# A two-stream scan kernel: the upper channels of the reverse stream convolved by taps on VectorE, b*s moved to GpSimd, one add of u, a new bank plan

## The chip, the cores and the metric

The kernel runs on one NeuronCore of one Trainium2 chip. The metric is the device time of one execution in microseconds (us), the median of several runs. The engines are called TensorE (PE in the profile, PEld its weight loads), VectorE (DVE), ScalarE (ACT) and GpSimd (POOL).

## The reference, cut to what matters

```python
# x: (4, 128, 96, 96) fp32; four sequences per image (rows and columns, each forwards and backwards)
t = grouped1x1(groupnorm(seq), in_proj)           # 4 groups, 128 -> 512 channels
u, gate = t[:, :256], t[:, 256:]
u = depthwise_conv(silu(u), dw_w)                 # 5 taps along the sequence, 256 channels
s = ssm_in @ u                                    # 32 channels
a = clip(DMIN + (DMAX - DMIN) * sigmoid(delta @ u), 1e-4, 0.9999)    # DMIN 0.999, DMAX 0.9999
b, c = tanh(B @ u), tanh(C @ u)
h = scan(h * a + b * s)                           # along the sequence
u = u + ssm_out @ (c * h + d * s)
y = out_proj @ grouped1x1(u * sigmoid(gate), mix) # then summed over the four sequences by fuse
```

Everything is fp32.

## The kernel before

The forward and the reverse stream run side by side. A *step* is 16 rows of both streams, cut by position modulo 4; a *pair* is one of the four positions p of a step in both streams, 384 columns each. There are 192 pairs. Each engine has its fixed order of instructions in a pair; the back part (gate, output, sum) lags six pairs behind the front. The depthwise convolution is done in two ways: on TensorE with banded 128x32 weights, or *by taps*: one ScalarE and four VectorE operations on the shifted silu. Only one of the four half-streams (forward, channels 128 to 255) went by taps.

```python
def by_taps(s, j):                # s: stream, j: half of the 256 channels
    return s == 0 and j == 1

GATE, FRONT, CONV_R, Y_F, SMALL = (0, 1), (2, 3), (0, 1), 2, 3      # PSUM banks
SSM, PROJ, Y_R, CONV_F = (4, 6), (5, 4), 6, 7

def conv(un, j):                  # by band: 8 matmuls and a copy
    ...
    for k in range(2):
        for g in range(4):
            mm(pc, g, band[:, j, un["p"], k, g, :], sil[:, j, g, k : k + N], k == 0, k == 1)
    nc.scalar.copy(un["u"][:, j, :], pc[:, :N])

def taps(un, ks):                 # by taps
    ...
        if k == 0:
            nc.scalar.activation(part, src, AF.Copy, scale=w_tap[:, 0:1])
        else:
            nc.vector.scalar_tensor_tensor(
                part, src, w_tap[:, k : k + 1], part, ALU.mult, ALU.add)

def ssm_out(bi):                  # after the matmuls, for each stream:
    ...
        nc.vector.tensor_add(pz, pz, bu["u"])
        nc.vector.scalar_tensor_tensor(gv, gv, 1.0, pz, ALU.add, ALU.mult)

def inputs(i):                    # for the pair before
    nc.scalar.activation(ta[:, p, :], bank(PROJ[0])[:, :N], AF.Tanh, bias=b_proj[:, 0:1])
    nc.gpsimd.tensor_scalar(a, a, half, DMIN + half, ALU.mult, ALU.add)
    nc.gpsimd.tensor_scalar(a, a, 0.9999, 0.0001, ALU.min, ALU.max)
    nc.vector.tensor_mul(ta[0:64, p, :], bank(PROJ[1])[64:P, :N], ta[0:64, p, :])   # b*s

def outputs(step, p):             # c*h + d*s, and a copy to the other partitions
    nc.gpsimd.tensor_mul(ta[64:P, p, :], tb[0:64, p, :], ta[0:64, p, :])
    nc.gpsimd.tensor_add(tb[64:P, p, :], ta[64:P, p, :], tb[64:P, p, :])
    nc.gpsimd.tensor_copy(tb[0:64, p, :], tb[64:P, p, :])
```

Of the kernel before, what the change touches and what calls it, by code (L numbers as in the profile page):

```python
# [35 lines left out]
P = 128  # L36
# [7 lines left out]
R = 4  # L44
# [9 lines left out]
def conv_preact_kernel(  # L54
# [58 lines left out]


    psum = ps.tile([P, 8, 512], F32, name="psum")
    GATE, FRONT, CONV_R, Y_F, SMALL = (0, 1), (2, 3), (0, 1), 2, 3
    SSM, PROJ, Y_R, CONV_F = (4, 6), (5, 4), 6, 7

# [41 lines left out]
    def stats_finish(b):  # L160
# [27 lines left out]
        nc.vector.tensor_scalar_mul(bn[:, 2:4], bn[:, 2:4], 0.5)  # L188
        bs = sp.tile([P, 2, 4], F32, tag="bsilu", name=f"bsilu_{b}")
        for q in range(R):  # L190
            for g in range(4):
                nc.gpsimd.tensor_copy(
                    bs[32 * q : 32 * q + 32, :, g], bn[32 * g : 32 * g + 32, 0:2]
                )
# [51 lines left out]

    band = wp.tile([P, 2, R, 2, 4, 32], F32, name="band")
    w_fin = wp.tile([P, 4, 2, P], F32, name="w_fin")
    b_fin = wp.tile([P, 1], F32, name="b_fin")
    with tc.tile_pool(name="prep", bufs=1) as pp:  # L250
        w_dw = load(dw_v, [P, 2, 4, 8], "w_dw", pp)
        id32 = pp.tile([P, 32], F32, name="id32")
        ident = pp.tile([P, P], F32, name="ident")
        make_identity(nc, ident)
        for q in range(R):
            r = slice(32 * q, 32 * q + 32)
            nc.gpsimd.tensor_copy(id32[r, :], ident[r, r])
        for j in range(2):
            for p in range(R):
                for k in range(2):  # L260
                    for g in range(4):
                        m = R * k - p + R - 1
                        nc.gpsimd.tensor_scalar_mul(
                            band[:, j, p, k, g, :], id32, w_dw[:, j, g, m : m + 1]
                        )

# [50 lines left out]

    def by_taps(s, j):
        return s == 0 and j == 1

    sils = {}

    def rows(i, bi, front_banks=FRONT):

        if i is not None:
            step, k = divmod(i, UB)
            s, g = divmod(k, 4)
            un = units[step * UB + s]
            wn, bn, bsil = stats[un["b"]]
            if g == 0:  # L330
                sils[step, s] = wk.tile(
                    [P, 2, 4, N + 1], F32, tag=f"sil{s}", name=f"sil_{step}_{s}"
                )
            sil = sils[step, s]
        if bi is not None:
            bu = units[bi]
            gwn, gbn, _ = stats[bu["b"]]
            gq, off = gate_at(bu)
        for c in range(4):
            for j in range(2):  # L340
                if i is not None:
                    r = slice(32 * j, 32 * j + 32)
                    m, q = (c, g) if by_taps(s, j) else (g, c)
                    mm(bank(front_banks[j]), c, wn[r, 32 * m : 32 * m + 32], x_in[s][r, q, :],
                       True, True)
                if bi is not None:
                    r = slice(64 + 32 * j, 96 + 32 * j)
                    mm(bank(GATE[j]), c, gwn[r, 32 * c : 32 * c + 32],
                       x_in[bu["s"]][r, gq, off : off + N], True, True)
        if bi is not None:  # L350
            gv = wk.tile([P, 2, N], F32, tag="gv", name=f"gv_{bu['id']}")
            for j in range(2):
                nc.scalar.activation(  # L353
                    gv[:, j, :],
                    bank(GATE[j])[:, :N],
                    AF.Tanh,
                    bias=gbn[:, 2 + j : 3 + j],
                    scale=0.5,
                )
            load_gate(bi + UB)  # L360
            bu["v"] = gv
        if i is not None:
            for j in range(2):
                nc.scalar.activation(  # L364
                    sil[:, j, g, :],
                    bank(front_banks[j])[:, : N + 1],
                    AF.Silu,
                    bias=bn[:, j : j + 1] if by_taps(s, j) else bsil[:, j, g : g + 1],
                )
            if g == 3:  # L370
                for j in range(2):
                    tap = by_taps(s, j)
                    if un["st"] == 0:
                        r, q = (slice(0, P), slice(0, 2)) if tap else (slice(0, 64), slice(0, 4))
                        nc.gpsimd.memset(sil[r, j, q, 0:1], 0.0)
                    if un["st"] == NS - 1:
                        r, q = (slice(0, P), slice(2, 4)) if tap else (slice(64, P), slice(0, 4))
                        nc.gpsimd.memset(sil[r, j, q, N : N + 1], 0.0)
                load_front(step + 1, s)

    def ssm_out(bi):

        pair = units[bi], units[bi + 1]
        z, p = scans[pair[0]["step"]][1], pair[0]["p"]
        for c in range(4):
            for s in range(2):
                for j in range(2):
                    r = slice(64 * j + 32 * s, 64 * j + 32 * s + 32)
                    mm(bank(SSM[s] + j), c, w_so[r, 128 * j + 32 * c : 128 * j + 32 * c + 32],
                       z[r, p, :], True, True)  # L390
        for s, bu in enumerate(pair):
            pz, gv = psum[:, SSM[s] : SSM[s] + 2, :N], bu["v"]
            nc.vector.tensor_add(pz, pz, bu["u"])  # L393
            nc.vector.scalar_tensor_tensor(gv, gv, 1.0, pz, ALU.add, ALU.mult)  # L394

    def conv(un, j):
        sil = sils[un["step"], un["s"]]
        pc = bank(CONV_R[j] if un["s"] else CONV_F)
        for k in range(2):
            for g in range(4):  # L400
                mm(pc, g, band[:, j, un["p"], k, g, :], sil[:, j, g, k : k + N], k == 0, k == 1)
        nc.scalar.copy(un["u"][:, j, :], pc[:, :N])  # L402

    def new_u(un):
        un["u"] = wk.tile([P, 2, N], F32, tag="u", bufs=2 * LAG + 2, name=f"u_{un['id']}")

    def taps(un, ks):
        sil, j = sils[un["step"], un["s"]], 1
        for k in ks:
            off, q = divmod(un["p"] + k, R)  # L410
            src, part = sil[:, j, q, off : off + N], un["u"][:, j, :]
            if k == 0:
# [8 lines left out]

    def proj(i, which):

        un = units[i]
        step, p = un["step"], un["p"]
        if step not in scans:
# [4 lines left out]
        ta, tb = scans[step]  # L431
        pp = bank(PROJ[which])
        cols = (qb, qb, qa, qa) if which == 0 else (qc, qc, qs, qs)
        for j in range(2):
            for c in range(4):
                mm(pp, c, w_proj[:, j, cols[c]], units[i + c % 2]["u"][:, j, :], j == 0, j == 1)
        if which == 1:
            nc.scalar.activation(  # L438
                tb[0:64, p, :], pp[0:64, :N], AF.Tanh, bias=b_proj[0:64, 1:2]
            )  # L440
            nc.scalar.activation(tb[64:P, p, :], pp[64:P, :N], AF.Copy, scale=d_sb[64:P, :])

    def inputs(i):

        un = units[i]
        ta, p = scans[un["step"]][0], un["p"]
        nc.scalar.activation(ta[:, p, :], bank(PROJ[0])[:, :N], AF.Tanh, bias=b_proj[:, 0:1])  # L447
        a = ta[64:P, p, :]
        half = (DMAX - DMIN) / 2
        nc.gpsimd.tensor_scalar(a, a, half, DMIN + half, ALU.mult, ALU.add)  # L450
        nc.gpsimd.tensor_scalar(a, a, 0.9999, 0.0001, ALU.min, ALU.max)  # L451
        nc.vector.tensor_mul(ta[0:64, p, :], bank(PROJ[1])[64:P, :N], ta[0:64, p, :])  # L452

# [53 lines left out]
    def pair(t):  # L507
        i, k, bi = 2 * t, t % R, 2 * (t - LAG)
        conv_here = i < NU
        front = i + UB if i + UB < NU else None  # L510
        back = 0 <= bi < NU
        if 0 <= i - 2 < NU:
            inputs(i - 2)
        rows(front, bi if back else None)
        if 0 <= bi - 2 < NU:
            accumulate(units[bi - 1])
        if conv_here:
            conv(units[i], 0)
        if k < 2 and 0 <= t // R - 1 < NU // UB:
# [4 lines left out]
        if conv_here:  # L524
            un = units[i]
            if un["order"] == "V" and un["b"] + 1 < B:
                stats_chunk(un["b"] + 1, un["st"] * R + k)
                if un["st"] == NS - 1 and k == R - 1:
                    later[:] = [stats_finish(un["b"] + 1)]
        if front is not None or back:  # L530
            rows(None if front is None else front + 1, bi + 1 if back else None)
        if back:
            ssm_out(bi)
        if conv_here:
            new_u(units[i + 1])
            for j in range(2):
                conv(units[i + 1], j)
        if back:
            accumulate(units[bi])
        if later:  # L540
            next(later[0], None)
        if i + 2 < NU:
            new_u(units[i + 2])
            taps(units[i + 2], range(K))
        if conv_here:
            proj(i, 1)
            proj(i, 0)

    for _ in stats_finish(b0):
        pass  # L550
    for i in range(UB):
        rows(i, None, (2 * (i % 2), 2 * (i % 2) + 1))
    new_u(units[0])
    taps(units[0], range(K))
    with tc.manual_schedule(
# [73 lines left out]
```

## Time and profile before

| | before |
|---|---|
| median | 2466.55 us (3 runs, 2462.74 to 2468.8) |
| TensorE, VectorE, ScalarE, GpSimd busy | 97%, 76%, 64%, 43% |
| four pairs | 49.2 us (order V: the sequences along the columns), 47.8 us (order H: along the rows) |

The busy shares, the chain and the costliest groups are shown in the prediction. One more view: the waits of GpSimd and of VectorE in the kernel before (who waited for whom: us in total, times, longest).

```profile
POOL t L450 <- ACT t L447: 1190.2, 189, 15.0
DVE psum L393 <- PE psum L314: 247.5, 133, 3.6
DVE t L465 <- POOL t L451: 18.5, 48, 1.0
```

GpSimd stands idle for 1190 us until ScalarE's tanh comes, and VectorE waits for TensorE ahead of the add of u.

### The profile page before, as it was taken

Reading aid. Unit: us, or ns where it says so; the run is one execution under the profiler, and the core shown is the slowest. Engines: PE = TensorE matmul, PEld = TensorE weight load, DVE = VectorE, ACT = ScalarE, POOL = GpSimd, SP = SyncE. Lnnn points to the kernel's source line nnn. Section 1 sums busy time; section 2 is a strip of 40 time slices with the busy share of each in tenths; the row PEclk is TensorE's granted clock in tenths of the full one; section 3 lists DMA queues with packets and bytes.
Section 4 is the critical chain, followed back from the end, with each engine's and each line's share of the span. In section 5 each row is a group of like instructions: output and inputs, shape, how many; then the busy total and the mean of one; then the engine's idle time right before and its main releaser. Section 6 shows DMA issues by size and latency. Waiting matters only on the chain.

```text
span 2461.1 us, 89876 instructions
## 1 busy us (share of the span) xinstructions
PE 2389.1 (97%) x40016; PEld 913.3 (37%) x40016; DVE 1859.2 (76%) x2343; ACT 1572.8 (64%) x2912; POOL 1051.3 (43%) x1170
## 2 busy tenths in 40 slices
PE   6999999999999999999999999999999999999997
PEld 3333333333333333333333333333333333333331
DVE  3688777777887787777877788777777777777774
ACT  4666676666666666666665666666666666666641
POOL 4344444444444444444443444444443444444441
PEclk9999999999999999999999999999999999999997
DMA  5212111113332211111342211111232111111111
GB/s 140 56 47 54 47 41 32 38 31 89 98 100 52 54 44 34 35 38 31 93 139 55 54 46 41 31 38 31 52 120 89 31 38 33 38 31 38 25 45 56
DMA packets 79283, 134.21 MB, mean 55 GB/s; under 512 B 11440, under 2 KB 73392, under 8 KB 78896
## 3 DMA queue, kind: packets, MB, share of 16 engines
q1 hardware_dynamic: 76704, 127.64, 19.3%
q8 instruction: 314, 5.14, 0.9%
q10 hardware_dynamic: 2192, 0.83, 0.1%
q14 instruction: 73, 0.60, 0.1%
HBM read 109.55 MB, written 18.87 MB: 52 GB/s over the span
## 4 chain that ended last, share of the span: by engine, by line
PE 82%; DVE 9%; POOL 3%; ACT 3%; issue 1%; DMA 0%; DVEq 0%; SPq 0%
PE psum L314 82%; DVE t L465 4%; ACT t L447 2%; DVE gv L394 2%; DVE psum L393 2%; POOL t L450 1%; POOL t L451 1%; DVE u L415 0%; DMA out<-acc 0%; DVE bn L310 0%; DMA acc<-in_xr 0%; ACT gv L353 0%; ACT L364 0%; ACT L438 0%; ACT sil L364 0%
## 5 line engine op out<-in xcount | busy, mean ns | idle before, releaser
L314 PE MATMUL psum<-sil,band 128*32 128x384 f32 x9216 | 821.6, 488 | 0.0
L450 POOL TENSOR_SCALAR t<-t 64x384 f32<-64x384 f32 x192 | 186.3, 970 | 1190.4 <-ACT t L447 1190.2
L314 PE MATMUL psum<-gv,w_fin 128*32 128x384 f32 x6144 | 582.9, 497 | 31.0 <-DVE gv L394 29.0
L393 DVE TENSOR_TENSOR psum<-psum,u 128x768 f32<-128x768 f32 x384 | 369.3, 962 | 248.3 <-PE psum L314 247.5
L314 PE MATMUL psum<-u,w_proj 128*32 128x384 f32 x6144 | 533.0, 486 | 0.0
L415 DVE SCALAR_TENSOR_TENSOR u<-sil,w_tap,u 128x384 f32<-128x384 f32 x768 | 478.9, 624 | 56.9 <-ACT u L413 35.7
L353 ACT ACTIVATE gv<-psum,bnorm 128x384 f32<-128x384 f32 x768 | 403.7, 577 | 153.2 <-PE psum L314 153.2
L402 ACT COPY u<-psum 128x384 f32<-128x384 f32 x576 | 276.0, 479 | 339.3 <-PE psum L314 339.3
L314 PEld LDWEIGHTS psum<-sil,band 128*32 128x32 f32 x9216 | 284.0, 109 | 489.7 <-issue 344.9
L314 PE MATMUL psum<-x_in,wn 32*32 32x385 f32 (+1 forms) x12288 | 389.9, 502 | 13.3 <-DVE acc L490 8.5
L394 DVE SCALAR_TENSOR_TENSOR gv<-gv,psum 128x768 f32<-128x768 f32 x384 | 366.5, 955 | 43.7 <-ACT sil L364 0.9
L314 PEld LDWEIGHTS psum<-gv,w_fin 128*32 128x32 f32 x6144 | 183.5, 110 | 388.7 <-issue 289.6
L364 ACT ACTIVATE sil<-psum,bsilu 128x385 f32<-128x385 f32 x576 | 314.6, 586 | 5.6 <-PE psum L314 5.4
L438 ACT ACTIVATE t<-psum,b_proj 64x384 f32<-64x384 f32 x192 | 110.6, 576 | 321.7 <-PE psum L314 263.8
L314 PEld LDWEIGHTS psum<-u,w_proj 128*32 128x32 f32 x6144 | 211.9, 110 | 280.2 <-issue 276.6
L472 POOL TENSOR_TENSOR t<-t,t 64x384 f32<-64x384 f32 x192 | 289.1, 1506 | 15.0
L471 POOL TENSOR_TENSOR t<-t,t 64x384 f32<-64x384 f32 x192 | 249.5, 1300 | 95.9 <-DVE t L465 85.9
L314 PE MATMUL psum<-t,w_so 32*32 32x384 f32 x6144 | 256.2, 493 | 2.9 <-DVE t L452 2.9
L452 DVE TENSOR_TENSOR t<-psum,t 64x384 f32<-64x384 f32 x192 | 179.4, 934 | 103.9 <-ACT t L447 103.0
L447 ACT ACTIVATE t<-psum,b_proj 128x384 f32<-128x384 f32 x192 | 208.6, 1087 | 25.3 <-PE psum L314 2.3
L314 PEld LDWEIGHTS psum<-x_in,wn 32*32 32x32 f32 x12288 | 99.3, 104 | 275.3 <-ACT sil L364 129.9
L451 POOL TENSOR_SCALAR t<-t 64x384 f32<-64x384 f32 x192 | 184.9, 963 | 15.9
(62 smaller groups left out, 1166.5 us busy)
## 6 DMA issues: line engine op xcount, KB each, us to landing
x_in<-in_xs SPq DMA_DIRECT2D x96, 385.0 KB, 4.4
x_in<-in_xs SPq DMA_DIRECT2D x384, 96.2 KB, 2.6
out<-acc SPq DMA_DIRECT2D x24, 768.0 KB, 4.9
xs<-in_xr SPq DMA_DIRECT2D x72, 192.0 KB, 2.4
acc<-in_xr SPq DMA_DIRECT2D x18, 768.0 KB, 4.9
acc<-in_xr SPq DMA_DIRECT2D x24, 192.0 KB, 3.6
w_fuse<-in_fuse_wT ACTq DMA_DIRECT2D x1, 256.0 KB, 4.8
w_proj<-in_proj_wT ACTq DMA_DIRECT2D x1, 128.0 KB
```

The costliest lines, as they stand in the source:

```text
L314: nc.tensor.matmul(o[r, : rhs.shape[-1]], lhsT, rhs, start=start, stop=stop, skip_group_check=True)
L353: nc.scalar.activation(gv[:, j, :], bank(GATE[j])[:, :N], AF.Tanh, bias=gbn[:, 2 + j : 3 + j], scale=0.5,)
L364: nc.scalar.activation(sil[:, j, g, :], bank(front_banks[j])[:, : N + 1], AF.Silu, bias=bn[:, j : j + 1] if by_taps(s, j) else bsil[:, j, ...
L393: nc.vector.tensor_add(pz, pz, bu["u"])
L394: nc.vector.scalar_tensor_tensor(gv, gv, 1.0, pz, ALU.add, ALU.mult)
L402: nc.scalar.copy(un["u"][:, j, :], pc[:, :N])
L415: nc.vector.scalar_tensor_tensor(part, src, w_tap[:, k : k + 1], part, ALU.mult, ALU.add)
L447: nc.scalar.activation(ta[:, p, :], bank(PROJ[0])[:, :N], AF.Tanh, bias=b_proj[:, 0:1])
L450: nc.gpsimd.tensor_scalar(a, a, half, DMIN + half, ALU.mult, ALU.add)
L451: nc.gpsimd.tensor_scalar(a, a, 0.9999, 0.0001, ALU.min, ALU.max)
L471: nc.gpsimd.tensor_mul(ta[64:P, p, :], tb[0:64, p, :], ta[0:64, p, :])
L472: nc.gpsimd.tensor_add(tb[64:P, p, :], ta[64:P, p, :], tb[64:P, p, :])
```

## The change

The intent: TensorE is the bound, so the second of the four half-streams leaves it and goes by taps. VectorE is relieved in return: b*s goes to GpSimd, which needs a ScalarE copy of s out of PSUM, and the adds of u of both streams become one, for which four neighbouring banks are needed. The accumulation of the forward stream moves behind the projections, and two of the new taps are put off to the next pair. The diff, cut to its core:

```diff
-    GATE, FRONT, CONV_R, Y_F, SMALL = (0, 1), (2, 3), (0, 1), 2, 3
-    SSM, PROJ, Y_R, CONV_F = (4, 6), (5, 4), 6, 7
+    FIRST = ((2, 3), (1, 7))
+    Y_R, CONV_F = 4, 1
+    SECOND = ((6, 7), (4, 5))
+    SSM = 0
+    CONV_R, PROJ, Y_F, SMALL = 4, (5, 6), 0, 7
 ...
-    def by_taps(s, j):
-        return s == 0 and j == 1
 ...
+        pz = psum[:, SSM : SSM + 4, :N]
+        nc.vector.tensor_add(pz, pz, us[bi].rearrange("p s j n -> p (s j) n"))
         for s, bu in enumerate(pair):
-            nc.vector.tensor_add(pz, pz, bu["u"])
-            nc.vector.scalar_tensor_tensor(gv, gv, 1.0, pz, ALU.add, ALU.mult)
+            nc.vector.scalar_tensor_tensor(
+                bu["v"], bu["v"], 1.0, pz[:, 2 * s : 2 * s + 2, :], ALU.add, ALU.mult
+            )
 ...
+        st = wk.tile([P, N], F32, tag="s", name=f"s_{i}")
+        nc.scalar.copy(st[0:64, :], pb[64:P, :])
 ...
-        nc.vector.tensor_mul(ta[0:64, p, :], bank(PROJ[1])[64:P, :N], ta[0:64, p, :])
+        nc.gpsimd.tensor_mul(ta[0:64, p, :], st[0:64, :], ta[0:64, p, :])
 ...
         if conv_here:
-            conv(units[i], 0)
+            conv(i, 0)
+            if i:
+                taps(i, 1, range(3, K))
 ...
         if conv_here:
-            new_u(units[i + 1])
-            for j in range(2):
-                conv(units[i + 1], j)
-        if back:
-            accumulate(units[bi])
+            conv(i, 1)
+        if i + 2 < NU:
+            new_u(i + 2)
+            taps(i + 2, 0, range(K))
+            taps(i + 2, 1, range(1))
+        if conv_here:
+            proj(i)
+        if back is not None:
+            accumulate(units[bi])
+        if i + 2 < NU:
+            taps(i + 2, 1, range(1, 3))
```

In VectorE's order a pair is now: add to acc (reverse), two put-off taps, scan (in two of four pairs), one add of u, two gates, four taps, add to acc (forward), two taps. Line numbers shift: the taps are L415 before and L420 after, the add of u L393 and L389, b*s L452 and L450, the first operation of the outputs L471 and L469.

## The prediction

> **What bounds the kernel now.** I read the page first: busy shares, then the chain that ended last, then the costliest groups.
>
> ```profile
> PE 2389.1 (97%) x40016; PEld 913.3 (37%) x40016; DVE 1859.2 (76%) x2343; ACT 1572.8 (64%) x2912; POOL 1051.3 (43%) x1170
> PE 82%; DVE 9%; POOL 3%; ACT 3%; issue 1%; DMA 0%; DVEq 0%; SPq 0%
> L314 PE MATMUL psum<-sil,band 128*32 128x384 f32 x9216 | 821.6, 488 | 0.0
> L393 DVE TENSOR_TENSOR psum<-psum,u 128x768 f32<-128x768 f32 x384 | 369.3, 962 | 248.3 <-PE psum L314 247.5
> L415 DVE SCALAR_TENSOR_TENSOR u<-sil,w_tap,u 128x384 f32<-128x384 f32 x768 | 478.9, 624 | 56.9 <-ACT u L413 35.7
> L402 ACT COPY u<-psum 128x384 f32<-128x384 f32 x576 | 276.0, 479 | 339.3 <-PE psum L314 339.3
> L452 DVE TENSOR_TENSOR t<-psum,t 64x384 f32<-64x384 f32 x192 | 179.4, 934 | 103.9 <-ACT t L447 103.0
> L471 POOL TENSOR_TENSOR t<-t,t 64x384 f32<-64x384 f32 x192 | 249.5, 1300 | 95.9 <-DVE t L465 85.9
> ```
>
> TensorE is busy 97% and is 82% of the chain; DVE waits for it at L393. The loop runs 192 pairs (a position p of both streams), and TensorE sets their pace: in the timeline of DVE, L452 of successive pairs without a scan stands at 1234.71, 1246.77 and 1258.86, so 12.06 us a pair. Of four pairs two carry a scan; scans of part 0 lie at 1211.76 and 1260.96 (49.2 us for four pairs, order V), and at 2347.53 and 2395.30 (47.8 us, order H). The mean is 12.1 us a pair.
>
> Then I asked what DVE's taps (L415) cost when GpSimd works beside them, since the change doubles them. The timeline of DVE and GpSimd, first an ordinary pair, then the pair at a change of phase, where the two happen to coincide:
>
> ```profile
> 1243.67 2.57 DVE L415 SCALAR_TENSOR_TENSOR u<-sil,w_tap,u 128x384 f32<-128x384 f32 x4
> ...
> 702.23 0.90 POOL L450 TENSOR_SCALAR t<-t 64x384 f32<-64x384 f32 x1 [6.70 <-ACT t L447]
> 702.64 5.12 DVE L415 SCALAR_TENSOR_TENSOR u<-sil,w_tap,u 128x384 f32<-128x384 f32 x4
> 703.22 1.11 POOL L451 TENSOR_SCALAR t<-t 64x384 f32<-64x384 f32 x1
> 704.39 1.41 POOL L471 TENSOR_TENSOR t<-t,t 64x384 f32<-64x384 f32 x1
> 705.88 1.47 POOL L472 TENSOR_TENSOR t<-t,t 64x384 f32<-64x384 f32 x1
> 707.41 0.71 POOL L473 COPY t<-t 64x384 f32<-64x384 f32 x1
> ```
>
> Four taps take 5.12 us in place of 2.57, and each GpSimd operation some 0.17 to 0.22 us more: they take turns. In narrower windows the taps start at 702.64, 703.57 and 704.74 and the third ends at 706.21, so a tap beside a TENSOR_SCALAR has a period of 1.17 us and beside a TENSOR_TENSOR about 1.5, against 0.64 alone: **+0.53 us for each TENSOR_SCALAR, +0.86 us for each TENSOR_TENSOR** that falls among taps. Today it hardly ever happens, as GpSimd stands idle while taps run (it waits 1190 us for L447).
>
> **What the Trainium skill says.** "SBUF — State Buffer", section "Who interferes with whom": a DVE instruction with two SBUF inputs contends with a GpSimd instruction that reads SBUF, and one with at most one SBUF input does not; the second to issue blocks. The trace agrees on both: the taps and the scan (sil with u, a with b) are stretched, while the add of u (PSUM and SBUF) stays at 0.95 to 0.97 us beside GpSimd. It agrees less on "the whole instruction": the tap that follows ends 0.37 us after L451, under its own 0.62, so the ports come free some 0.25 us before GpSimd's end. "GPSIMD Engine Reference", section "4.1 Engine selection", advises VectorE for elementwise work and calls two-input operations about 2 times slower on GpSimd; here the uncontended multiply L471 takes 1.24 us, the DVE multiply L452 0.93, so 1.3 times. "Trainium Kernel Development and Optimization", section "Key Constraints": GpSimd cannot access PSUM; hence the new ScalarE copy of s.
>
> **The change part by part.** TensorE: the banded convolution of the reverse stream's upper half goes, 3072 of the 9216 instructions in the first group: 821.6/3 = 274 us, 1.43 us busy a pair, some 1.30 us of pace (two convolutions cover 1213.83 to 1216.44). 12.06 - 1.30 = 10.76 us a pair if TensorE still set it; busy 2115 us.
>
> DVE: four more taps a pair, +768 x 0.624 = +479 us. The multiply L452 leaves, -179. The two adds of 768 become one of 1536: 768 cost 0.962, 384 (acc, L490) 0.557, so 768 more cost 0.81 and one add 1.77 against 1.92: -30. Sum 1859 + 270 = 2129 us, without waits at the ports.
>
> ScalarE: a tap start (0.619) for a copy (0.479), and the copy of s (some 0.48): +0.62 us a pair, 1692 us; not the bound. GpSimd: a multiply of 1.24 us, +238; some 6.1 us a pair in series: two TENSOR_SCALAR, the new multiply, then two TENSOR_TENSOR and a copy of the outputs.
>
> **Pace after, without contention.** From the distances of starts in the DVE timeline, work of a pair without a scan: two adds to acc 1.0, eight taps 4.9, add 1.88 to the next start, two gates 1.74: 9.5 us. The scans add 1.93 each, bn_stats 0.47 in the V half. DVE is then ahead in pairs without a scan (TensorE: 10.8) and sets the pace of those with one (11.5 to 12): some 11.4 a pair.
>
> **Pace after, with contention.** GpSimd's first operation waits for ScalarE's tanh, and that for the projections, which end 4.0 us after ssm_out; tanh takes 1.1. So GpSimd starts 5.2 us after the add of u could start. DVE has then done the add and the gates (3.6 us, which take no shared port) and is at the third of its next four taps. All six GpSimd operations thus fall among taps: the two TENSOR_SCALAR and b*s on the end of these four and the two after accumulate, the outputs on the two deferred taps of the next pair. In us from the start of the add (a tap holds the ports some 0.47, a TENSOR_SCALAR 0.70, a TENSOR_TENSOR 1.03, read from the ends in that pair): taps at 3.6, 4.3 and 4.9; GpSimd's first gets in at 5.4, the fourth tap goes at 6.1 in place of 5.5 (0.53); the second TENSOR_SCALAR at 6.5 runs beside the add to acc, and the next tap goes at 7.25 in place of 7.1 (0.16); b*s at 7.7 holds the last tap until 8.75 (0.86); the outputs' multiply at 9.2 holds the first deferred tap until 10.25 after acc at 9.3 to 9.8 (0.48), their add at 10.7 the second until 11.75 (0.86). Together 0.53 + 0.16 + 0.86 + 0.48 + 0.86 = 2.9 us. A pair without a scan is then 9.5 + 2.9, some **12.3 to 12.8 us, and DVE is the bound**. The pair with scan part 0: 12.3 + 1.93 + some 0.1 = 14.3. In the pair with part 1 the outputs wait for the scan and then run beside the add and gates for nothing: 9.5 + 1.95 + 2.0 = 13.4. Four pairs: 14.3 + 13.4 + 12.8 + 12.3 = 52.8, and bn_stats in half of them adds 0.7: 53.5, 13.4 a pair against 12.1.
>
> Of 192 pairs 186 have a back part: 186 x 1.25 = +232 us. The first six get a little shorter (TensorE's 1.3 us each), the last six some 0.8 us longer (the longer add is in their chain): together nothing. 2466 + 232 = 2698. About 39 us of stalls of TensorE in the kernel before, outside these regular pairs (span less start 47, first six 51, 186 x 12.1 and tail 69), should partly vanish beside a busier DVE: I take **2660 us**.
>
> **The rivals.** One: DVE and GpSimd do not collide, the phase shifts so that outputs run beside the add and gates. Then 11.4 a pair and 2466 - 186 x 0.7 = some 2335 us. For it: GpSimd has 5 us idle a pair and the add and gates are free of ports. Against it: its input comes late in every pair, by data. Two: TensorE stays the bound with the whole saving, 10.76 a pair, some 2210 us. Against it: DVE's 2129 us of work leave no room for waits, and scans bunch in two of four pairs. Three: half the waits occur, 12.4 a pair: 2500 us, near a tie. Four: ScalarE, in order, holds back the projections, as its tap starts wait for the add of u (the buffer of u comes free there): another 0.2 to 0.5 us a pair, 2740 us; with 9.9 us of work in 13 it has room.
>
> **Range and chances.** The turn-taking is seen, not assumed, but only in a few places, and my order of events can slip by one operation (0.5 to 0.9 us a pair, 90 to 160 us). Hence 2520 to 2780. Slower 0.82; within 2%, as in rival three, 0.09; faster, as in rivals one and two, 0.09.
>
> **What would show it.** Right: DVE busy over 93%, TensorE near 80%; taps' mean not 624 but some 950 ns (1536 x 0.33 more makes 2.6 us a pair); GpSimd's two-input mean near 1.4 us; waits of TensorE for DVE acc and gv; the chain mostly DVE. Wrong: taps at 0.62 to 0.7 us with DVE idle before the add of u, or ScalarE named in the waits of TensorE. The prediction fails if GpSimd's block slides into the add and gates, or if the lock is lighter than in that one pair.

## The result, and the profile after

The changed kernel takes 2767.41 us (median of 4 runs, 2757.45 to 2767.48) against 2464.64 us. A ratio here is the mean time of one kernel's fast runs over that of the other's of the same rounds, so not quite the ratio of the medians: 1.122, 95% interval 1.1186 to 1.1254. It is slower by 12%.

The page of the changed kernel: busy time (share of the span, instructions), the chain that ended last, and groups (busy us, mean ns, then idle time before).

```profile
PE 2378.9 (86%) x36944; PEld 824.1 (30%) x36944; DVE 2545.7 (92%) x2727; ACT 1630.1 (59%) x3104; POOL 1385.6 (50%) x1330
DVE 72%; PE 8%; issue 4%; ACT 1%; DMA 0%; DVEq 0%
L420 DVE SCALAR_TENSOR_TENSOR u<-sil,w_tap,u 128x384 f32<-128x384 f32 x1536 | 1488.2, 969 | 49.5 <-ACT u L418 13.6
L389 DVE TENSOR_TENSOR psum<-psum,u 128x1536 f32<-128x1536 f32 x192 | 337.7, 1759 | 82.9 <-ACT sil L362 47.8
L450 POOL TENSOR_TENSOR t<-s,t 64x384 f32<-64x384 f32 x192 | 272.2, 1418 | 14.5
L469 POOL TENSOR_TENSOR t<-t,t 64x384 f32<-64x384 f32 x192 | 259.7, 1353 | 279.3 <-DVE t L463 263.7
```

The chain has turned from TensorE (82% before) to VectorE (72%). The taps are twice as many, as intended, but each now takes 969 ns in place of 624. GpSimd's two-input operations, 1.24 us when nothing meets them, have means of 1.35 and 1.42. Both engines are called busy while they wait for each other, so no wait of VectorE shows in the waits.

The timeline shows the turns: VectorE and GpSimd in one pair with the second scan part, and the start of the next (start, length, engine, line).

```profile
1212.05 1.77 DVE L389 TENSOR_TENSOR psum<-psum,u 128x1536 f32<-128x1536 f32 x1
1213.85 1.82 DVE L391 SCALAR_TENSOR_TENSOR gv<-gv,psum 128x768 f32<-128x768 f32 x2
1215.59 4.67 DVE L420 SCALAR_TENSOR_TENSOR u<-sil,w_tap,u 128x384 f32<-128x384 f32 x4
1220.18 0.60 DVE L493 SCALAR_TENSOR_TENSOR acc<-psum,b_fin,acc 128x384 f32<-128x384 f32 x1
1220.71 2.46 DVE L420 SCALAR_TENSOR_TENSOR u<-sil,w_tap,u 128x384 f32<-128x384 f32 x2
1223.57 1.26 DVE L420 SCALAR_TENSOR_TENSOR u<-sil,w_tap,u 128x384 f32<-128x384 f32 x2
...
1212.10 1.22 POOL L469 TENSOR_TENSOR t<-t,t 64x384 f32<-64x384 f32 x1 [5.69 <-DVE t L463]
1213.39 1.24 POOL L470 TENSOR_TENSOR t<-t,t 64x384 f32<-64x384 f32 x1
1214.70 0.50 POOL L471 COPY t<-t 64x384 f32<-64x384 f32 x1
1215.97 1.23 POOL L448 TENSOR_SCALAR t<-t 64x384 f32<-64x384 f32 x1 [0.77 <-ACT t L441]
1217.28 1.06 POOL L449 TENSOR_SCALAR t<-t 64x384 f32<-64x384 f32 x1
1218.42 1.42 POOL L450 TENSOR_TENSOR t<-s,t 64x384 f32<-64x384 f32 x1
1219.92 1.39 POOL L469 TENSOR_TENSOR t<-t,t 64x384 f32<-64x384 f32 x1
```

From 1212.1 to 1215.2 GpSimd works beside the add and the gates, and both engines take their undisturbed times. From 1216 on it works beside taps: four take 4.67 us in place of 2.57, and the next two, which meet the outputs of the following pair (L469), 2.46 in place of 1.26. The two put-off taps at 1223.57 meet nothing and take 1.26.

### The profile page after: what moved, and what is told of

It is laid out like the page before. It is cut to its first block, busy times and chain, and to the rows that moved or that the text cites. A ratio compares the mean times of both kernels' runs of the same rounds, so it can differ in the third digit from the quotient of the medians.

```text
span 2765.8 us, 83353 instructions
## 1 busy us (share of the span) xinstructions
PE 2378.9 (86%) x36944; PEld 824.1 (30%) x36944; DVE 2545.7 (92%) x2727; ACT 1630.1 (59%) x3104; POOL 1385.6 (50%) x1330
## 4 chain that ended last, share of the span: by engine, by line
DVE 72%; PE 8%; issue 4%; ACT 1%; DMA 0%; DVEq 0%
DVE u L420 42%; DVE gv L391 11%; DVE psum L389 10%; PE psum L315 8%; DVE acc L488 3%; DVE t L463 2%; DVE acc L493 2%; DVE acc L495 2%; DVE bn L311 1%; ACT gv L351 1%; ACT sil L362 0%; DMA acc<-in_xr 0%; DMA out<-acc 0%; DVE wn L184 0%; ACT u L405 0%
## 5 line engine op out<-in xcount | busy, mean ns | idle before, releaser
L420 DVE SCALAR_TENSOR_TENSOR u<-sil,w_tap,u 128x384 f32<-128x384 f32 x1536 | 1488.2, 969 | 49.5 <-ACT u L418 13.6
L315 PE MATMUL psum<-x_in,wn 32*32 32x385 f32 (+1 forms) x12288 | 538.1, 515 | 314.0 <-DVE acc L488 148.3
L448 POOL TENSOR_SCALAR t<-t 64x384 f32<-64x384 f32 x192 | 225.9, 1177 | 943.0 <-ACT t L441 942.9
L315 PE MATMUL psum<-sil,band 128*32 128x384 f32 x6144 | 619.2, 523 | 4.0 <-ACT gv L351 3.9
L389 DVE TENSOR_TENSOR psum<-psum,u 128x1536 f32<-128x1536 f32 x192 | 337.7, 1759 | 82.9 <-ACT sil L362 47.8
L469 POOL TENSOR_TENSOR t<-t,t 64x384 f32<-64x384 f32 x192 | 259.7, 1353 | 279.3 <-DVE t L463 263.7
L315 PE MATMUL psum<-t,w_so 32*32 32x384 f32 x6144 | 389.1, 580 | 0.9 <-ACT u L405 0.9
L315 PEld LDWEIGHTS psum<-sil,band 128*32 128x32 f32 x6144 | 189.6, 116 | 408.0 <-issue 222.1
L450 POOL TENSOR_TENSOR t<-s,t 64x384 f32<-64x384 f32 x192 | 272.2, 1418 | 14.5
L418 ACT ACTIVATE u<-sil,w_tap 128x384 f32<-128x384 f32 x384 | 215.5, 609 | 100.2 <-DVE psum L389 99.5
L362 ACT ACTIVATE sil<-psum,bnorm 128x385 f32<-128x385 f32 x384 | 227.2, 592 | 0.0
```

Of the source, the lines that this page charges most:

```text
L315: nc.tensor.matmul(o[r, : rhs.shape[-1]], lhsT, rhs, start=start, stop=stop, skip_group_check=True)
L362: nc.scalar.activation(sil[:, j, g, :], bank(banks[0][j])[:, : N + 1], AF.Silu, bias=bn[:, 1:2] if j else bsil[:, g : g + 1],)
L389: nc.vector.tensor_add(pz, pz, us[bi].rearrange("p s j n -> p (s j) n"))
L420: nc.vector.scalar_tensor_tensor(part, src, w_tap[:, k : k + 1], part, ALU.mult, ALU.add)
L450: nc.gpsimd.tensor_mul(ta[0:64, p, :], st[0:64, :], ta[0:64, p, :])
```

## The experiments

Three theories were set against each other. **A, turns at the ports:** taps and scan take two inputs from SBUF and must take turns with GpSimd's reads, which makes VectorE the bound. **B, too much work:** VectorE's own work and its fixed order are too long in any case. **C, the bank plan:** TensorE's second rows need bank 4, which VectorE must have emptied by its add to acc; TensorE waits for that, and its clock falls. The waits of the changed kernel speak for C at first sight:

```profile
PE psum L315 <- DVE acc L488: 148.3, 76, 3.6
PE psum L315 <- DVE acc L495: 142.2, 71, 3.6
```

Each run was timed in rounds with the kernel before on one chip. The runs lie on four chips, on which the kernel before took 2460.5 to 2465.6 us:

| run | what | median us | ratio to before (95%) |
|---|---|---|---|
| the change | | 2767.4 | 1.122 (1.1186 to 1.1254) |
| e1_no_reads | GpSimd writes only, memsets three times over | 2775.8 | 1.1259 (1.1237 to 1.128) |
| e1b_single | GpSimd writes only, one memset each | 2272.4 | 0.9216 (0.9198 to 0.9235) |
| e2_outputs_no_reads | only the outputs as memsets | 2578.4 | 1.0458 (1.043 to 1.0486) |
| e3_gate | outputs held back beside the add | 2601.1 | 1.0554 (1.0537 to 1.0572) |
| e4_bs_on_vector | b*s back on VectorE | 2831.7 | 1.1487 (1.1462 to 1.1511) |
| e5_band_back | the band back, poor bank | 2697.6 | 1.0962 (1.0945 to 1.0979) |
| e5b_band_back | the band back, mended | 2463.0 | 0.9995 (0.9967 to 1.0023) |
| e6_bs_alone | before, with b*s on GpSimd | 2539.5 | 1.0321 (1.0304 to 1.0339) |
| e7_bank | reverse sum in bank 0 | 2798.2 | 1.1367 (1.135 to 1.1384) |
| e8_gate_no_clip | gate, and no clip | 2530.6 | 1.0282 (1.0258 to 1.0306) |
| e9_affine_on_scalar | and a*half + middle on ScalarE | 2432.7 | 0.9869 (0.9849 to 0.9889) |
| e10_bs_gated | and b*s held back too | 2367.2 | 0.961 (0.9595 to 0.9624) |

### e1_no_reads and e1b_single: GpSimd without reads

Their outputs are wrong, which doesn't matter for the times. The comparison with the reference still passed, so it doesn't see errors of this size in the scan branch: weak evidence for this part in any version.

```diff
-        nc.gpsimd.tensor_scalar(a, a, half, DMIN + half, ALU.mult, ALU.add)
-        nc.gpsimd.tensor_scalar(a, a, 0.9999, 0.0001, ALU.min, ALU.max)
-        nc.gpsimd.tensor_mul(ta[0:64, p, :], st[0:64, :], ta[0:64, p, :])
+        nc.gpsimd.memset(a, 0.9995)                  # e1: each three times
+        nc.gpsimd.memset(a, 0.9995)
+        nc.gpsimd.memset(ta[0:64, p, :], 0.01)
 ...
-        nc.gpsimd.tensor_mul(...); nc.gpsimd.tensor_add(...); nc.gpsimd.tensor_copy(...)
+        for part in (ta[64:P, p, :], tb[64:P, p, :], tb[0:64, p, :]):
+            nc.gpsimd.memset(part, 0.01)             # e1: each three times
```

> Wrong result on purpose: each of GpSimd's six operations of a pair becomes three memsets of the same tile, so GpSimd writes but reads nothing; order, waits, banks, DVE, ScalarE and TensorE are unchanged. Theory A (turns at the ports: taps and scan of DVE wait for GpSimd's reads, 2.6 to 3 us a pair): taps back to 0.62 to 0.66 us, some 11.4 us a pair, 2340 us (2280 to 2420). Theory B (DVE simply has too much work of its own, 2129 us plus gaps in a fixed order): 2700 us or more. Theory C (the new bank plan: bank 4 is shared by the sum of the reverse stream and the gates of the second rows, so TensorE waits for DVE's add to acc, 290 us in the waits, and its clock falls): the wait stays, over 2600 us.

Measured: 2775.8 us, as slow as the change, a miss for theory A's time. But the page of this run shows why: the taps are at their undisturbed length, and it is the scan that now waits.

```profile
PE 2292.2 (83%) x36944; PEld 807.7 (29%) x36944; DVE 2011.4 (73%) x2727; ACT 1628.1 (59%) x3104; POOL 2427.5 (88%) x3634
L420 DVE SCALAR_TENSOR_TENSOR u<-sil,w_tap,u 128x384 f32<-128x384 f32 x1536 | 945.7, 616 | 92.2 <-ACT u L418 56.4
DVE t L466 <- POOL t L453: 422.1, 48, 10.9
```

Three memsets in place of one operation took 1.7 to 2.5 us, more than the operation, and GpSimd itself became the bound (88% busy, 57% of the chain). The test of the time was spoilt by its own size. What it does show: with GpSimd busier than ever, but only writing, a tap takes 616 ns. It isn't GpSimd's being busy that stretches taps, it is its reading.

> The first attempt mended: there the triple memsets (0.56 to 0.85 us each) kept GpSimd busy 88% and made it the new bound, though the taps fell to 616 ns. Now one memset in place of each of the six operations, some 4.2 us a pair, wrong values on purpose. Theory A (turns at the ports): taps stay at 0.62 us, DVE's own work and TensorE set the pace, 11.4 us a pair or a little less: 2330 us (2270 to 2400), faster than the kernel before. Theory B (DVE's own work is too much): 2600 us or more. Theory C (bank plan): TensorE still waits some 290 us for DVE's add to acc, over 2500 us.

Measured: 2272.4 us, 7.8% faster than the kernel before, 495 us less than the change. From its page and its waits:

```profile
PE 2190.9 (96%) x36944; PEld 809.2 (36%) x36944; DVE 2003.0 (88%) x2727; ACT 1627.7 (72%) x3104; POOL 844.0 (37%) x1330
L420 DVE SCALAR_TENSOR_TENSOR u<-sil,w_tap,u 128x384 f32<-128x384 f32 x1536 | 945.1, 616 | 53.8 <-ACT u L418 18.0
PE psum L315 <- DVE acc L487: 6.9, 3, 3.1
PE psum L315 <- DVE acc L494: 5.1, 8, 0.7
```

Theories B and C fall as the main cause: the order, the banks and VectorE's own work are those of the change, and yet TensorE is busy 96% again, and its 290 us of waits for acc have shrunk to 12 (6.9 and 5.1). Against the change the taps alone save 1488.2 - 945.1 = 543 us of VectorE's time. The run takes away GpSimd's reads and much of its time together (844 us busy against 1386); that nobody waits for GpSimd's results in the change (the scan waits 3 us for it in all, the 1.8 and 1.3 us of idle time before its two groups) makes the time itself an unlikely cause. What the runs show is that GpSimd's reads and VectorE's instructions with two SBUF inputs stretch each other; that it is a port which they share is what the prediction took over, and no run looks at the port itself.

### e2_outputs_no_reads and e3_gate: only the outputs

```diff
 # e2: the outputs' three operations become memsets, three times over
 # e3: the outputs stay, but wait for VectorE's put-off taps, or for the scan
         if 0 <= i - 10 < NU:
             d = units[i - 10]
+            if conv_here:
+                g = wk.tile([32, 1], F32, tag="gate", name=f"gate_{t}")
+                src = us[i][0:32, 1, 1, 0:1]
+                if k == 0:
+                    src = scans[t // R - 1][0][0:32, R - 1, N // 2 - 1 : N // 2]
+                nc.gpsimd.tensor_copy(g, src)
             outputs(d["step"], d["p"])
```

> Wrong result on purpose: only the three operations of the outputs become memsets; the two tensor_scalar and b*s stay. Theory A: the share of the outputs, 0.48 + 0.86 us in three of four pairs, goes: about 1.0 us a pair, 190 us, so 2570 us (2500 to 2620). Theories B and C: 2765 us, unchanged within 2%.

> Right result: the outputs are kept on GpSimd but a copy of one column of u (or of the scan's result) ahead of them makes GpSimd wait until DVE's deferred taps (or the scan) are done, so that the outputs run beside the add of u and the gates. Theory A: the same gain as without the reads of the outputs, 2570 us (2510 to 2630), the deferred taps at 0.62 us. Theory B: unchanged, 2765 us, or slower by the added wait. Theory C: unchanged.

Measured: 2578.4 and 2601.1 us, where A expected 2570 for both and B and C no gain. e3 does all the work of the change and one more small copy a pair, and it is 166 us faster because GpSimd *waits*. Its timeline, GpSimd and VectorE in one pair:

```profile
1206.61 1.22 POOL L469 TENSOR_TENSOR t<-t,t 64x384 f32<-64x384 f32 x1
1207.91 1.23 POOL L470 TENSOR_TENSOR t<-t,t 64x384 f32<-64x384 f32 x1
...
1207.23 1.77 DVE L389 TENSOR_TENSOR psum<-psum,u 128x1536 f32<-128x1536 f32 x1 [0.91 <-PE psum L315]
1210.77 3.72 DVE L420 SCALAR_TENSOR_TENSOR u<-sil,w_tap,u 128x384 f32<-128x384 f32 x4
...
1217.06 1.26 DVE L420 SCALAR_TENSOR_TENSOR u<-sil,w_tap,u 128x384 f32<-128x384 f32 x2
```

The outputs run beside the add at their undisturbed 1.22 us, the put-off taps (1217.06) are back at 1.26 us for two, and the four taps still pay (3.72), as the two tensor_scalar and b*s meet them as before.

### e4_bs_on_vector: one part undone

```diff
-        st = wk.tile([P, N], F32, tag="s", name=f"s_{i}")
-        nc.scalar.copy(st[0:64, :], pb[64:P, :])
 ...
-        nc.gpsimd.tensor_mul(ta[0:64, p, :], st[0:64, :], ta[0:64, p, :])
 ...
         if back is not None:
             accumulate(units[bi])
+        if conv_here:
+            ta, p = scans[units[i]["step"]][0], units[i]["p"]
+            nc.vector.tensor_mul(ta[0:64, p, :], bank(PROJ[1])[64:P, :N], ta[0:64, p, :])
```

> One part undone: b*s goes back from GpSimd to DVE, read from PSUM, ahead of the last two taps, and ScalarE's copy of s goes. Theory A: DVE gains 0.93 us of work a pair and loses a turn of 0.86 us: within 2% of 2765 us. Theory B: 192 x 0.93 = 179 us more, 2940 us. Theory C: 2765 us or a little more.

Measured: 2831.7 us, 2.3% above the change, just outside what A expected and well below B's 2940. In the balance of VectorE, A holds: its busy time is 2554.1 us against 2545.7, so the multiply's added 0.92 us a pair are given back by taps of 855 in place of 969 ns. The 64 us are not isolated. A likely place is a new wait: TensorE waits 96 us for this multiply, which frees a bank of the projections late in VectorE's order (the wait named `DVE t L541` of this run). Moving b*s to GpSimd was not the mistake of the change.

### e5_band_back and e5b_band_back: the main part undone

The reverse half goes back to the band with a band and a layout of silu as in the kernel before; all other parts stay.

```diff
         if conv_here:
-            conv(i, 1)
+            conv(i, 1, 1)          # e5: upper half first, into bank 7
+            conv(i, 1)             # e5b: the other way round, and the projections
+                                   #      take the halves in the order 0, 1
 ...
-            taps(i + 2, 1, range(1))
-        if i + 2 < NU:
-            taps(i + 2, 1, range(1, 3))
-                taps(i, 1, range(3, K))
```

> The main part undone alone: the reverse stream's channels 128 to 255 go back to the band on TensorE; b*s on GpSimd, the one add of u, the bank plan and the order of accumulate stay. Theory A: only four taps a pair are left, of which the last two meet GpSimd's two tensor_scalar; DVE has some 8.1 us plus scans, TensorE 12.06 us a pair sets the pace again: 2440 us (2400 to 2490). Theory C (the bank plan costs): over 2600 us.

Measured: 2697.6 us, a clear miss. The waits of this run name a fault of the experiment: bank 7 still holds the rows that ScalarE empties last.

```profile
PE psum L316 <- ACT sil L366: 228.2, 187, 1.3
```

> The main part undone, mended: in the first attempt the returned convolution was put first into bank 7, which ScalarE had not yet emptied, and TensorE waited 228 us for that silu. Now it comes second and the projections take the halves in the old order. Theory A: the 228 us go, TensorE sets the pace with some 12.06 us a pair: 2450 us (2410 to 2500), a tie with the kernel before. Theory C (the bank plan itself costs): over 2550 us.

Measured: 2463.0 us, ratio 0.9995 (0.9967 to 1.0023): a tie with the kernel before. So the one add, the bank plan, b*s on GpSimd and the new order cost nothing together and gain nothing. The 12% come with the reverse stream's taps. With e1b this makes three corners of a square: band with reads 2463, taps with reads 2767, taps without reads 2272. More taps are good without the reads, and the reads cost no time while the reverse half is on the band; only both together are slow. The turns are there in e5b too (a tap takes 751 ns, 40 of the scans 2.68 us), but VectorE, busy 71%, has room for them. The fourth corner, band without reads, was not run.

### e6_bs_alone: one part alone, on the kernel before

```diff
+            st = wk.tile([P, N], F32, tag="s", name=f"s_{i}")
+            nc.scalar.copy(st[0:64, :], pp[64:P, :N])
 ...
-        nc.vector.tensor_mul(ta[0:64, p, :], bank(PROJ[1])[64:P, :N], ta[0:64, p, :])
+        nc.gpsimd.tensor_mul(ta[0:64, p, :], un["st_copy"][0:64, :], ta[0:64, p, :])
```

> One part alone, on the kernel before: b*s on GpSimd with ScalarE's copy of s, nothing else. Theory A: there GpSimd's operations start with the pair, while the taps stand at its end, so few meet; DVE loses work that was not the bound: 2465 us within 1.5%. Rival (b*s on GpSimd is itself what costs, by its 1.24 us ahead of the scan or its turns): 2500 us or more.

Measured: 2539.5 us, 3.2% slower; the rival was right here. The reason is not the taps (626 ns) but a plain wait, of the kernel before with this part:

```profile
DVE t L468 <- POOL t L455: 96.3, 48, 3.8
```

b*s is the third of GpSimd's operations in series ahead of the scan, and in the old order they begin only with the next pair, so the first scan part waits 2 us for it each time. What follows becomes late too: TensorE's waits for the gates behind the scan (`PE psum L314 <- DVE gv L394`) rise from 29.0 to 92.9 us. The change issues these operations in the pair of the projections themselves, and there this wait is gone. The part is harmful alone and neutral in its company, which the tie of e5b shows.

### e7_bank: theory C directly

```diff
-    Y_R, CONV_F = 4, 1
+    Y_R, CONV_F = 0, 1
```

> The sum of the reverse stream goes to bank 0 in place of bank 4, so that the second rows no longer wait for DVE's add to acc; the four banks of ssm_out wait for it instead, some 0.7 us later. Theory C: TensorE's waits for acc of 290 us mostly go and the time falls by 100 to 250 us. Theory A: DVE's own sequence with its turns at the ports is the bound, TensorE's waits are its result and turn up elsewhere: within 2% of 2765 us.

Measured: 2798.2 us, 1.1% slower than the change. TensorE's waits for acc did not go; they rose from 290 to 406 us. VectorE's order is late, and TensorE meets it at whichever bank it needs next. A wait in the list names a place, not a cause.

### e8, e9, e10: taking GpSimd's reads away from the taps

```diff
 # e8: e3 and
-        nc.gpsimd.tensor_scalar(a, a, 0.9999, 0.0001, ALU.min, ALU.max)
 # e9: e8 and
-        nc.gpsimd.tensor_scalar(a, a, half, DMIN + half, ALU.mult, ALU.add)
+        nc.scalar.activation(a, a, AF.Copy, bias=DMIN + half, scale=half)
 # e10: e9, but b*s of three pairs in four waits with the outputs of the next pair
+        if conv_here and i:
+            ...                                  # the gate as in e3, on the scan where k < 2
+            nc.gpsimd.tensor_copy(g, src)
+        if i - 2 in bs_of:
+            b_times_s(i - 2)
```

The clip can be left out because a lies between 0.999 and 0.9999 by its formula, but for a rounding.

> The gate of the outputs and one operation less on GpSimd: the clip of a is left out, as a lies between 0.999 and 0.9999 by its formula. Theory A: beside the gain of the gate (about 1.0 us a pair) another 0.2 to 0.5 us a pair: 2490 us (2430 to 2550), near the kernel before. Theories B and C: 2765 us.

> Right result, aimed at beating both: outputs gated, clip left out, and a = half*tanh + middle done by ScalarE, so that of GpSimd's operations only b*s can meet the taps. Theory A: some 0.4 us of waits in pairs without a scan and 0.85 in the others, about 11.8 us a pair: 2410 us (2350 to 2470), 2% faster than before. If ScalarE, with about 1 us more a pair, becomes the bound: 2500 us or more.

> Right result, built on the version with the affine step on ScalarE: in three of four pairs b*s too waits for the end of DVE's deferred taps (or the scan) of the next pair and runs ahead of the outputs, so that of GpSimd's 4.2 us only the copy of 0.5 us can still meet the first tap; only the b*s that the next scan needs stays where it was. Theory A (turns at the ports): in three pairs of four 0.45 to 0.85 us of turns go, 0.4 us a pair on the mean: 2360 us (2310 to 2410), taps' mean near 0.66 us. If the turns are no longer what sets the pace there (TensorE's 10.8 us a pair does): 2420 us or more.

Measured: 2530.6, 2432.7 and 2367.2 us. Each step that takes reads out of the taps' way pays within the range that A gave for it. e9: 1.3% faster than before; the last version beats both kernels: 3.9% faster than before and 14% below the change. It keeps all of the added taps. The taps and the add of u in it:

```profile
L420 DVE SCALAR_TENSOR_TENSOR u<-sil,w_tap,u 128x384 f32<-128x384 f32 x1536 | 1003.2, 653 | 58.8 <-ACT u L418 23.1 <-ACT sil L362 1.6
L389 DVE TENSOR_TENSOR psum<-psum,u 128x1536 f32<-128x1536 f32 x192 | 338.6, 1764 | 142.9 <-PE psum L315 130.9 <-ACT gv L351 9.9
```

A tap takes 653 ns, and VectorE waits for TensorE again. As the comparison is blind to errors of the size made in e1b, that e8 to e10 are right rests on their computing the same formula.

## Why the prediction was right

**That VectorE becomes the bound through turns with GpSimd** was the step that everything hung on, and it held: e1b removes the reads and the time falls by 495 us, e3 only moves some of them and it falls by 166.

**The cost of the turns** was put at 2.9 us in three pairs of four and 2.0 in the fourth, 2.7 on the mean. The taps of the change took (1488.2 - 945.1)/192 = 2.8 us a pair more than in e1b. The expected mean of some 950 ns was 969. GpSimd's two-input mean, expected near 1.4 us, was 1.35 to 1.42, but this sign could not have told right from wrong: the outputs' two such operations (L471, L472) already had 1.30 and 1.51 us in the kernel before, where they met the scan.

**Where the turns fall** was foreseen less well, and that the sum came out is in part luck. By the medians over the whole trace of the change, GpSimd's first operation starts 3.9, 4.0, 5.1 and 4.2 us after the add of u in the four pairs from scan part 1 on, where the steps had 5.2 to 5.4. So in three pairs of four its first three operations all meet the four taps, which lose some 2.1 us in place of 0.53. The put-off taps, for which 0.48 + 0.86 us were put down in three pairs of four, lose 1.3 us in one of them and nothing in the others, where the outputs meet the two taps before them, as in the timeline above. The sums of a pair are 2.2, 3.4, 3.1 and 3.4 us, against 2.0 and three times 2.9 in the prediction: the operations that met taps were about as many, but not the ones named.

**VectorE's own terms** held: the add of 1536 was put at 1.77 us and took 1.76; the copy of s at 0.48 and took 0.48. The sum of 2129 us was too high; e1b is busy 2003. Of the 126 us, 51 are scans: the sum took over those of the kernel before, of which 40, all of part 0, lasted 2.92 us because GpSimd's multiply got in first, and in the changed kernel the same scans take 1.83 us. Most of the rest is overlap: the records of neighbouring instructions of VectorE overlap by 42 us in the kernel before and by 100 us in e1b, and busy time counts an overlap once.

**One reading was not like for like:** the 1.3 times between GpSimd and VectorE sets GpSimd's multiply, with both inputs in SBUF, against b*s of VectorE, with one input in PSUM. A tap, with as many elements a partition and both inputs in SBUF, takes 0.62 us, and 1.24 is 2.0 times that. Nothing in the forecast rests on it.

**The pace of the pairs** came out unevenly. From the starts of the add of u at 1198.56, 1212.05, 1226.39, 1238.68 and 1253.31, the pair with scan part 1 took 13.5 us (13.4 foreseen), the next 14.3 (12.8; by the median of all such pairs 14.4), the next 12.3 (12.3), the one with part 0 14.6 (14.3). The second of these is the term that was mis-sized: its turns took some 0.5 us more than foreseen, and it has a wait of 1.57 us that was not foreseen at all. The timeline there shows TensorE and VectorE:

```profile
1223.70 0.61 PE L315 MATMUL psum<-x_in,wn 32*32 32x384 f32 x15 [2.90 <-DVE acc L495]
1224.16 2.12 PE L315 MATMUL psum<-t,w_so 32*32 32x384 f32 x31
1226.39 1.77 DVE L389 TENSOR_TENSOR psum<-psum,u 128x1536 f32<-128x1536 f32 x1 [1.57 <-ACT sil L362]
...
1223.70:1228.30 4.60, 4.60 (x78) 1.58 (x82) 2.96 (x4) 2.00 (x4) 0.00 (x0) 0.63 0.10 27
```

TensorE had stood 2.90 us waiting for VectorE's add to acc; in the 4.6 us after that its granted clock was 0.63 (last row: window, busy times by engine, clock), a matmul group of some 1.3 us (w_so, 1.28 us in the kernel before) took 2.1, and VectorE, already the bound, then waited 1.57 us for it. (The profile names ScalarE's silu as what ended this wait, but the group ended at 1226.28, 0.11 us before the add began.) My steps had this loop (add to acc, second rows, ssm_out, add of u) at full clock only. This is theory C's grain of truth: the waits of VectorE ahead of the add of u, for which the steps had nothing, come to 82.9 us, of the 107 us between 2660 and 2767 (the range ended at 2780). How much of them is due to the lower clock is not shown. The rest may be the 39 us that I had taken off for stalls of the old kernel; no run isolates those, and without them the steps had given 2698.

**The signs named in advance:** VectorE over 93% was 92%; the chain mostly VectorE was 72%; waits of TensorE for acc and gv are there. TensorE near 80% was 86%, in part because its matmuls count as busy for longer at a mean clock of 0.948, against 0.992 before; but in e1b too, at 0.982, it is busy 2191 us where 2115 were foreseen.

**The rivals:** TensorE staying the bound and ScalarE holding back the projections are not seen (ScalarE itself waits, 544 us for TensorE's gates alone; its tap starts do wait 99.5 us for the add of u, as rival four has it, but TensorE's matmuls wait only 3.9 us for ScalarE's tanh of the gates). The first rival, 2335 us with no turns, is what e1b made true by force, and it came out lower, at 2272 us: four pairs took 44.6 us there (add of u at 1200.65 and 1245.26), 11.2 a pair where I had put 11.4.

## What to carry to other kernels

Before moving work to an idle engine, ask which ports its operands use: "idle 57%" of GpSimd and 24% of VectorE were not free, because the operations given to them take turns, and the profile books such turns as busy time, not as waits. Look for one place in the old trace where the two meet by chance; the prediction read one of two such places, four taps of 768, and it was enough to foresee a large loss, though not which operations would meet. In e5b turns of the same kind cost no time, as VectorE was not the bound there. And where two engines collide, let the one off the critical path wait for a stretch in which the other has no such instruction: here that was worth 166 us (e3), the removal of an instruction after it 70 us (e8).

## What the Trainium skill lacked or had wrong

- "SBUF — State Buffer", section "Who interferes with whom": the rule itself held. With two SBUF inputs VectorE and a reading GpSimd took turns (taps 969 against 616 ns), a GpSimd that only writes did not disturb (616 ns with GpSimd busy 88%), and VectorE's one-input work was not disturbed (add of u 1.76 us in the change and in every variant of it). Its list of operations that take the shared pair names neither scalar_tensor_tensor nor the scan, though its rule for two SBUF inputs covers them, and both do: taps as above, 40 scans of part 0 2.92 us in the kernel before and 1.83 in the changed one.
- The same page, section "Summary: rules for kernel authors", has the second one to issue blocked until the first finishes. By the profile's times the turn passes on earlier: the tap after a TENSOR_SCALAR ended 0.37 us after it, less than its own 0.62, and four taps with three GpSimd operations wholly among them took 5.12 us, while the undisturbed lengths of the taps (2.57) and of L451, L471 and L472 (0.95 + 1.24 + 1.23) add up to 6.0. The profile's spans of GpSimd are rough, so the end of an instruction there need not be the end of its reads, and a contradiction is not shown.
- No page that I found gives the price of a turn to a short dependent chain: +0.53 us for each TENSOR_SCALAR and +0.86 us for each TENSOR_TENSOR of 64x384 among taps of 0.64 us, read from one place of the kernel before, nor that the profile counts it as busy time of both engines.
- "GPSIMD Engine Reference", section "4.1 Engine selection", puts two-input operations at about 2 times VectorE's time. Against a tap with both inputs in SBUF this holds (1.24 to 0.62 us); against the multiply with one input in PSUM, 0.93 us, it is 1.3 times. The page does not tell the two apart.
- "TensorE: Matmul & The Clock Gate", Part 1, on the HAM clock gate, has the clock fall after an idle window of about 3.4 us; here a stand of 2.90 us by the profile was followed by 4.6 us at a granted clock of 0.63. The matmuls' ends are modelled, so the two need not contradict each other.
